# A graph network on one core: the stores of a sort's steps spread over its stream, the node figures' distance raised by one place, and the order of the first part left to the scheduler

## The chip, the cores and the metric

The kernel runs on one core of a Trainium2 chip. The time is the device time of one execution in microseconds; lower is better. Engines are named as the profile names them: PE is TensorE, DVE is VectorE, ACT is ScalarE, POOL is GpSimd, SP is SyncE. SP issues all of this kernel's transfers.

## What is computed

The input is sixteen graphs of N = 1024 nodes with C = 64 columns each, x, and an adjacency adj of 1024 by 1024. Four layers follow each other, each with a residual and a normalisation over the 64 columns. The first one costs nearly everything: it thins the adjacency ("dilation"), and then takes for every node and every column three quantiles over the node's remaining neighbours, with weights.

```python
def _dilate_adj(adj, mask):
    nb = (adj_ > 0) & (~eye)[None]
    m = nb.sum(-1)
    rank = jnp.cumsum(nb, axis=-1) - 1
    skip = jnp.where(m > T_THRESH, (m + K_DIL - 1) // K_DIL, 1)
    removed = nb & do_dil[..., None] & ((rank + 1) % skip[..., None] == 0)
    rem = removed | jnp.swapaxes(removed, 1, 2)
    return jnp.where(rem, 0.0, adj_)
...
for tau, wt in zip([0.25, 0.5, 0.75], [0.25, 0.5, 0.25]):
    pos = jnp.clip(tau * (mf - 1.0), 0.0)
    lo, hi = floor(pos), ceil(pos)
    q = gather(lo) * (1.0 - frac) + gather(hi) * frac     # of the sorted neighbours
    agg = agg + wt * q
...
x = _layernorm(x + _L0_gnn_ref(x, adj, nodemask, ...), axis=-1)
x = _layernorm(x + _L1_gnn_ref(x, adj, ...), axis=-1)      # three rounds of adj^T (x W)
x = _layernorm(x + _L2_gnn_ref(x, adj, ...), axis=-1)      # adj x / degree
x = _layernorm(x + _L3_gnn_ref(x, adj), axis=-1)           # (adj + I) x / sum
```

## The kernel before

**How the quantiles are found.** The kernel sorts the 1024 values of each column once and then counts: for six wanted ranks of each node it finds, by matmuls of the thinned adjacency with words that encode each value's place, in which block of 16 sorted values the rank falls, and then which value within it. The work unit (`Unit`) is one group of eight columns' words and one half of the nodes. A graph has 8 groups and 2 halves, so 16 units, and each unit has S = 6 turns, one for each wanted rank. In a turn VectorE makes a mask `mt` and a product `pr` (`masks`), TensorE sums them (`pw`, then `pr_`, `pv`, `fc`), ScalarE evacuates. Meanwhile TensorE counts for the next unit (`x` from `vt` and the words `xw`) and makes the next words (`pa` from `prow`). At the end of a group `total` reduces with the matmuls `p<-wv`.

**What runs beside it.** Four kinds of other work are written as Python generators, with a `yield` between their steps:

- `sort_pair` sorts the columns of two graphs at once (two graphs of 64 columns fill the 128 partitions). It is a bitonic network of 55 steps on VectorE; each step makes the comparison `m`, stores it to DRAM (`swaps`) and makes min and max. Then it takes differences of the sorted values ("the steps"), as float16 and a remainder, into a tile `both`, and stores that tile to DRAM with eight transfers (line 419). Then it lays out 0 to 1023 with an iota `ii` (line 427), copies it to `sr`, and runs the 55 steps backward, with each `m` loaded again, so that `sr` ends as the rank of each value. Those ranks become the rows that the words are made of.
- `dilate` thins one graph's adjacency: for each of eight tiles a threshold and a prefix sum (`sc`), six small POOL operations for the node figures `sk` (lines 515 to 520), two ACT passes that use `sk`, three VectorE operations; then transposes, row sums (`pm`) and the six ranks per node (`rd`).
- `degrees` sums the columns, by ACT, through one buffer `ac`.
- `layers` does the rest of the network for the graph before, with loads `a` of 512 KB through three buffers.

**What sets the order.** The main loop goes over `y`, one turn at a time, and each turn has two places. `Spread` puts the generators' steps into the places. A generator with so many `steps` between `first` and `end` has an even schedule, and `late` says how many places it is behind. `ready` lets a step wait until it is four places late (`LATE`) as long as VectorE's planned work, `Ordered.through`, is more than `BUSY` ahead of the place's time, `Ordered.now`; the kernel adds a fixed formula per VectorE instruction to `through`. A digit in what a generator yields is a distance: the next step comes at least so many places after this one. Letters: "p" is a use of TensorE, "v", "n", "h" limit which steps may share a place.

`Ordered` also chains each instruction of VectorE and ScalarE to the one written before it, without a wait, as `link` does for TensorE, so that their order is as written. SP and POOL aren't chained, and the scheduler of the framework orders them. While `Ordered.on` is false, VectorE and ScalarE are ordered by that scheduler too, and `through` isn't counted.

**The first part.** Before the main loop the first sort, the dilation of graph 0, its rows and its first words must be done. `Ordered.on` is set to true ahead of them. Dilation goes on by one step at every second step of the backward sort, and then at each word part.

**Buffers.** All tiles of a sort (`sv`, `both`, `ii`, `sr`, `sb`) share one tag with two buffers, and so `sr` is given the buffer of `both`; `m` has two buffers of its own.

```python
        both = sorts.tile([P, 2 * N], F16, tag="s", name="sv")
...
        ii, _, _ = slot("ii")
...
        _, r, d = slot("sr")
        V.tensor_copy(r, ii)
```

Of the kernel before, what the change touches and what calls it, by code (L numbers as in the profile page):

```python
# [37 lines left out]
def gnn_stack(  # L38
# [322 lines left out]
    def sort_pair(b, rows, found):  # L361
# [52 lines left out]
        for u in range(TURN):  # L414
            for c2 in range(2):
                q0 = (u * 2 + c2) * (C // 2)
                for i in range(2):

                    nc.sync.dma_start(
                        out=xs[u].rearrange("(b e) q i c f -> e i c q b f", e=2)[c2, i, c2],  # L420
                        in_=both[q0 : q0 + C // 2, ts(i, N)].rearrange("q (b f) -> q b f", f=F),
                    )
        found.append((xs, back))
        yield
        ii, _, _ = slot("ii")
        ii = ii.bitcast(I32)
        nc.gpsimd.iota(ii, pattern=[[1, N]], base=0, channel_multiplier=0)
# [51 lines left out]
    def dilate(g, found):  # L479

        mk = small.tile([P, T], F32, tag="mk", name="mk")
        V.tensor_copy(mk, mask8[:, g, :])
        den = small.tile([P, 2, T], F32, tag="den", name="den", bufs=3)
        vt = graph.tile([P, T, N], F16, tag="vt", name="vt", bufs=2)

        def block_of(t):
            a = []
            for h in range(2):
                a.append(strm.tile([P, HALF], F32, tag="da", name="da", bufs=2))
                nc.sync.dma_start(out=a[h], in_=adj[g, ts(t, P), ts(h, HALF)])  # L490
            return a

        a = block_of(0)
        yield
        for t in range(T):
            sc = dil.tile([P, 2 * N], F16, tag="d", name="sc")
            nb, cum = sc[:, 0:N], sc[:, N : 2 * N]
            q = vt[:, t, :]
            for h in range(2):
                V.tensor_scalar(nb[:, ts(h, HALF)], a[h], 0.0, None, ALU.is_gt)  # L500
                A.activation(
                    q[:, ts(h, HALF)], a[h], AF.Copy, accum_out=den[:, h, t : t + 1]
                )
            if t + 1 < T:
                a = block_of(t + 1)
            V.tensor_tensor(nb[:, ts(t, P)], nb[:, ts(t, P)], offdiag, ALU.mult)

            V.tensor_tensor_scan(cum, nb, nb, 0.0, ALU.add, ALU.max)
            yield
            m = cum[:, N - 1 : N]  # L510


            sk = small.tile([P, 5], F32, tag="sk", name="sk")
            G = nc.gpsimd
            G.tensor_scalar(sk[:, 0:1], m, 0.5, 0.5, ALU.add, ALU.mult)  # L515
            G.tensor_scalar(sk[:, 0:1], sk[:, 0:1], MAGIC, -MAGIC, ALU.add, ALU.add)
            G.tensor_scalar(sk[:, 1:2], m, T_THRESH, mk[:, t : t + 1], ALU.is_gt, ALU.mult)
            G.tensor_scalar(sk[:, 2:3], sk[:, 0:1], 1.0, sk[:, 1:2], ALU.add, ALU.mult)
            G.tensor_scalar(sk[:, 3:4], sk[:, 2:3], -1.5, 1.5, ALU.mult, ALU.add)
            G.tensor_scalar(sk[:, 4:5], sk[:, 2:3], 0.5, -0.5, ALU.mult, ALU.add)  # L520
            yield "4"

            for h in range(2):
                A.activation(
                    q[:, ts(h, HALF)], cum[:, ts(h, HALF)], AF.Abs, bias=sk[:, 3:4]
                )
                yield "2"
            V.tensor_scalar(q, q, sk[:, 4:5], 0.25, ALU.is_equal, ALU.max)
            V.tensor_tensor(q, q, nb, ALU.mult)
            V.scalar_tensor_tensor(  # L530
                q[:, ts(t, P)], ident16, 0.25, q[:, ts(t, P)], ALU.mult, ALU.add
            )
            yield
        yield

        tiles = vt.rearrange("p j (t m) -> p j t m", m=P)
        for j in range(T):
            for t0 in range(j + 1, T, 4):
                yield PEV
                n = min(4, T - t0)  # L540
                pq = bank(ps_l, "pq", dt=F16).rearrange("p (i t m) -> p i t m", i=2, m=P)
                for i in range(n):
                    transpose(pq[:, 0, i], tiles[:, t0 + i, j], ident16)
                    transpose(pq[:, 1, i], tiles[:, j, t0 + i], ident16)
                for i, side in enumerate((tiles[:, j, t0 : t0 + n], tiles[:, t0 : t0 + n, j])):
                    V.scalar_tensor_tensor(
                        side, pq[:, i, 0:n], 0.25, side, ALU.is_equal, ALU.is_gt
                    )
        yield PEV
        pq = bank(ps_l, "pq", dt=F16).rearrange("p (t m) -> p t m", m=P)  # L550
        for j in range(T):
            transpose(pq[:, j], tiles[:, j, j], ident16)
        side = bass.AP(vt.tensor, vt.offset, [list(vt.ap[0]), [N + P, T], [1, P]])
        V.scalar_tensor_tensor(side, pq, 0.25, side, ALU.is_equal, ALU.is_gt)
        yield

        rd = dram.tile([S, N], F16, name="rd")
        wd = dram.tile([S, N], F16, name="wd")
        yield PEV
        pm = bank(ps_l, "pm")  # L560
        for t in range(T):
            for j in range(T):
                matmul(
                    pm[:, t : t + 1], lhsT=vt[:, j, ts(t, P)], rhs=one16[:, 0:1],
                    start=(j == 0), stop=(j == T - 1), skip_group_check=True,
                )

        def wide_of(i):
            return by_s[:, i].unsqueeze(1).to_broadcast([P, T, S])

        pos = small.tile([P, T, S], F32, tag="pos", name="pos", bufs=1)
        nb1 = small.tile([P, T], F32, tag="nb1", name="nb1", bufs=1)
        rw = small.tile([P, T, 2 * S], F16, tag="rw", name="rw", bufs=1)
        r, w = rw[:, :, 0:S], rw[:, :, S : 2 * S]
        V.tensor_scalar(nb1, pm[:, 0:T], -1.0, 0.0, ALU.add, ALU.max)
        V.tensor_tensor(pos, nb1.unsqueeze(2).to_broadcast([P, T, S]), wide_of(0), ALU.mult)
        V.tensor_scalar(r, pos, 1023.625, 1024.0, ALU.add, ALU.max)
        V.scalar_tensor_tensor(pos, pos, 1024.0, r, ALU.add, ALU.subtract)
        V.tensor_tensor(w, pos, wide_of(1), ALU.mult)
        V.tensor_tensor(w, w, wide_of(2), ALU.add)  # L580
        V.scalar_tensor_tensor(pos, pos, 0.0, wide_of(3), ALU.is_gt, ALU.mult)
        V.tensor_tensor(r, r, pos, ALU.add)
        yield "4" + PEN
        pq = bank(ps_l, "pq", dt=F16)
        for t in range(T):
            transpose(pq[0 : 2 * S, ts(t, P)], rw[:, t], ident16)
        sc = dil.tile([P, 2 * N], F16, tag="d", name="sc")
        A.copy(sc[0 : 2 * S, 0:N], pq[0 : 2 * S])
        nc.sync.dma_start(out=rd, in_=sc[0:S, 0:N])
        nc.sync.dma_start(out=wd, in_=sc[S : 2 * S, 0:N])  # L590
        found.append((vt, rd, wd, den))
# [480 lines left out]
            )  # L1072
        infos[g]["w96"] = w96

    Ordered.on = True
    sorting, dilating = sort_of(0, sorted_), dilate(0, parts)
    for i, _ in enumerate(sorting):
        if i == 0:  # L1080
            onerow = strm.tile([P, N], F32, tag="a", name="onerow").bitcast(F16)[0:C, 0:N]
            V.memset(onerow, 1.0)
            for r in rows_in:
                nc.sync.dma_start(out=r[4], in_=onerow)
            nothing = strm.tile([P, N], F32, tag="a", name="nothing").bitcast(F16)
            V.memset(nothing, 0.0)
            for r in steps_in:
                for u in range(TURN):
                    nc.sync.dma_start(
                        out=r[u].rearrange("p q i c f -> p (q i c f)"), in_=nothing  # L1090
                    )
        if i > n_sort and i % 2:
            next(dilating, None)
    load_rows(rows_of(0), 0)
    load_rows(rows_of(0), 1)
    words = {0: {}}
    for k in range(KC):
        words[0][k] = wts.tile([P, 2, T, P], F16, tag="xw", name="xw")
        for part in range(4):
            word_part(0, words[0][k], k, part)  # L1100
            next(dilating, None)
            if part % 2:
                word_end(words[0][k], part // 2)
            next(dilating, None)
    all_of(dilating)
    info(0)
    for s in range(S):
        load_rank(0, s)
# [70 lines left out]
    for y in range(n_units * S + S):  # L1179
# [4 lines left out]
        if running and z == 0:  # L1184
# [2 lines left out]
            base = 2 * SLOTS * g  # L1187
            if g == 0 and TURN < B:
                background.append(
                    Spread(sort_of(1, sorted_), 2 * n_sort + 8, 0, base + 2 * SLOTS + ROWS)  # L1190
                )
            if g + 1 < B:
                background.append(Spread(dilate(g + 1, parts), 64, base, base + 168))
# [33 lines left out]
        for half in range(2):  # L1227

            if running:
# [3 lines left out]
                if g % TURN and place == base + ROWS and g + 3 < B:  # L1233

                    background.append(
                        Spread(
                            sort_of((g + 3) // TURN, sorted_), 2 * n_sort + 8, place,
                            place + 4 * SLOTS,
                        )
                    )  # L1240
# [74 lines left out]
```

## Time and profile before

| | us |
|---|---|
| median of three runs | 9303.98 (9301.11 to 9304.25) |
| the profiled execution | 9303.79 |
| its span, first to last instruction | 9302.0 |
| PE busy | 8584.0 |
| DVE busy | 8194.6 |
| ACT busy | 7165.3 |
| POOL busy | 1064.4 |

The mean granted clock of TensorE is 0.990. In the profile, a group is named by what it writes and reads (`pr<-mt,dw`), with the buffer numbers left out. Nearly all operations of VectorE and ScalarE carry the line of the helper in `Ordered` (L299) and those of TensorE that of `link`'s callers (L280, L277), so they are told apart by their tiles. A wait is given with the instruction that stood idle, what ended its idle time, the total in us, how often, and the longest. An instruction in order of time has its start, its length, and in brackets the idle time ahead of it. A row of a stretch of time has the busy time of PE, PEld, DVE, ACT and POOL with the number of instructions, then the granted clock, the DMA share and GB/s.

The sixteen graphs are spread evenly: with the matmuls `p<-wv` as marks, the second to the fourteenth graph take 546.7 to 559.8 us each.

### The profile page before, as it was taken

Reading aid. Unit: us, or ns where it says so; the run is one execution under the profiler, and the core shown is the slowest. Engines: PE = TensorE matmul, PEld = TensorE weight load, DVE = VectorE, ACT = ScalarE, POOL = GpSimd, SP = SyncE. Lnnn points to the kernel's source line nnn. Section 1 sums busy time; section 2 is a strip of 40 time slices with the busy share of each in tenths; the row PEclk is TensorE's granted clock in tenths of the full one; section 3 lists DMA queues with packets and bytes.
Section 4 is the critical chain, followed back from the end, with each engine's and each line's share of the span. In section 5 each row is a group of like instructions: output and inputs, shape, how many; then the busy total and the mean of one; then the engine's idle time right before and its main releaser. Section 6 shows DMA issues by size and latency. Waiting matters only on the chain.

```text
span 9302.0 us, 188268 instructions
## 1 busy us (share of the span) xinstructions
PE 8584.0 (92%) x78785; PEld 3692.7 (40%) x78785; DVE 8194.6 (88%) x8786; ACT 7165.3 (77%) x12465; POOL 1064.4 (11%) x923
## 2 busy tenths in 40 slices
PE   0689999999999999999999999999999999999997
PEld 0234444444444444444444444444444444444442
DVE  8799989989899998989999898998989899777663
ACT  0588878878787887878888787887878788887873
POOL 0110101101020110201112010210102111010000
PEclk9999999999999999999999999999999999999998
DMA  3111222222222222222222222222222222221111
GB/s 93 53 39 42 78 88 66 81 70 92 76 77 69 77 75 83 82 78 64 92 68 87 76 78 80 73 77 72 94 73 80 69 72 81 67 66 65 44 62 56
DMA packets 531942, 678.39 MB, mean 73 GB/s; under 512 B 234576, under 2 KB 349392, under 8 KB 531088
## 3 DMA queue, kind: packets, MB, share of 16 engines
q1 hardware_dynamic: 531088, 666.35, 23.4%
q8 instruction: 616, 10.09, 0.4%
q14 instruction: 238, 1.95, 0.1%
HBM read 584.36 MB, written 81.80 MB: 72 GB/s over the span
## 4 chain that ended last, share of the span: by engine, by line
PE 62%; DVE 22%; ACT 7%; issue 7%; DMA 1%; POOL 1%; SPq 1%; another core or an unknown queue 0%; DVEq 0%; POOLq 0%; ACTq 0%
PE x L280 27%; PE pa L280 10%; PE pw L280 9%; PE pv L280 7%; DVE pr L299 6%; DVE mt L299 5%; PE fc L280 3%; DVE sr L299 3%; ACT dw L299 3%; DVE sv L299 2%; DVE vt L299 1%; PE p L280 1%; ACT xw L299 1%; DVE sc L299 1%; DVE m L299 1%
## 5 line engine op out<-in xcount | busy, mean ns | idle before, releaser
L280 PE MATMUL x<-vt,xw 128*128 128x512 f16 x16384 | 3988.9, 381 | 102.7 <-ACT dw L299 99.4
L299 DVE TENSOR_TENSOR pr<-mt,dw 128x4096 f16<-128x4096 f16 x1536 | 3520.5, 2292 | 72.5 <-ACT dw L299 1.0
L299 DVE TENSOR_TENSOR mt<-cc,rB 128x2048 f16<-128x2048 f16 x1536 | 1871.6, 1218 | 677.4 <-PE pv L280 651.3
L280 PEld LDWEIGHTS <-xw 128*128 128x128 f16 x16384 | 1500.7, 98 | 1727.9 <-issue 419.0
L299 ACT ACTIVATE qq<-pw,col,icol 128x512 f16<-128x512 f32 x1536 | 1212.1, 789 | 776.4 <-PE pw L280 744.7
L299 ACT ACTIVATE xw<-pa 128x512 f16<-128x512 f32 x2048 | 1247.3, 609 | 471.2 <-PE pa L280 470.5
L299 ACT ACTIVATE dw<-x 128x512 f16<-128x512 f32 x2048 | 1119.3, 604 | 279.2 <-PE x L280 270.2
L299 ACT ACTIVATE xw<-xw 128x1024 f16<-128x1024 f16 x1024 | 1088.7, 1063 | 11.0
L280 PE MATMUL pa<-words_by,prow 128*128 128x128 f16 x8192 | 805.7, 221 | 306.8 <-DMA prow<-rows 283.1
L280 PEld LDWEIGHTS <-prow 128*128 128x128 f16 x8192 | 557.4, 98 | 1161.5 <-issue 670.0
L280 PE MATMUL pw<-pr,red 128*32 128x512 f16 x12288 | 932.4, 380 | 45.9 <-DVE pr L299 45.8
L299 ACT ACTIVATE val<-pv 128x512 f32<-128x512 f32 x1536 | 938.0, 611 | 6.4 <-PE x L280 5.0
L280 PE MATMUL pv<-mt,txw 128*32 128x512 f16 x12288 | 933.0, 380 | 0.0
L755 POOL TENSOR_TENSOR rstd<-var,neghalf 128x8 f32<-128x8 f32 x112 | 212.5, 1897 | 4223.2 <-DVE var L299 4223.2
L299 ACT ACTIVATE cc<-x 128x512 f16<-128x512 f32 x1024 | 613.2, 599 | 92.1 <-PE x L280 88.0
L280 PE MATMUL pw<-rB,subr 128*32 128x512 f16 x6144 | 615.2, 390 | 0.6 <-ACT qq L299 0.3
L299 DVE TENSOR_TENSOR sr<-sr 128x512 f16<-128x512 f16 x1336 | 598.6, 477 | 17.4
L280 PE MATMUL pv<-nt,nbig 128*32 128x512 f16 x6144 | 599.9, 380 | 0.0
L299 DVE TENSOR_TENSOR sv<-sv 128x512 f32<-128x512 f32 (+3 forms) x904 | 595.1, 698 | 0.6
L280 PE MATMUL fc<-val,fin 128*32 128x512 f32 x3072 | 528.0, 593 | 0.0
L515 POOL TENSOR_SCALAR sk<-sc 128x1 f32<-128x1 f16 x128 | 84.9, 663 | 3386.9 <-DVE sc L299 2310.7
L280 PEld LDWEIGHTS <-txw 128*32 128x32 f16 x12288 | 330.8, 97 | 335.0 <-issue 2.9
(3288 smaller groups left out, 8421.7 us busy)
## 6 DMA issues: line engine op xcount, KB each, us to landing
a<-adj_dram SPq DMA_DIRECT2D x360, 512.0 KB
a<-adjT_dram SPq DMA_DIRECT2D x240, 512.0 KB
da<-adj_dram SPq DMA_DIRECT2D x256, 256.0 KB
ac<-adjT_dram SPq DMA_DIRECT2D x256, 256.0 KB
swaps<-m SPq DMA_DIRECT2D x440, 128.0 KB
m<-swaps SPq DMA_DIRECT2D x440, 128.0 KB
rB<-rd SPq DMA_DIRECT2D x96, 256.0 KB
prow<-rows SPq DMA_DIRECT2D x512, 20.0 KB
```

Source lines behind the costliest of these rows:

```text
L280: link("PE", nc.tensor.matmul(*args, **kw))
L299: ins = call(*args, **kw)
L515: G.tensor_scalar(sk[:, 0:1], m, 0.5, 0.5, ALU.add, ALU.mult)
L755: nc.gpsimd.tensor_tensor(rstd, var, neghalf, ALU.pow)
```

## The change

There are three parts.

1. In `sort_pair` each pair of stores of `both` is followed by a `yield`, so that the eight stores make four steps in place of one, and the step with the iota comes with a distance of "4" behind the last pair. The number of steps that `Spread` reckons with goes from 2 n_sort + 8 to 2 n_sort + 12 (n_sort is 55).
2. In `dilate` the distance behind the node figures goes from "4" to "5", and the end of a tile gets a distance of "1".
3. In the first part, `Ordered.on` isn't set ahead of the sort (the main loop sets it), the first sort runs through, the first dilation is written behind it as a whole, and the word parts come without steps of dilation among them.

```diff
@@ sort_pair
                         in_=both[q0 : q0 + C // 2, ts(i, N)].rearrange("q (b f) -> q b f", f=F),
                     )
+                yield
         found.append((xs, back))
-        yield
+
+        yield "4"
         ii, _, _ = slot("ii")
@@ dilate
-            yield "4"
+            yield "5"
...
-            yield
+            yield "1"
         yield
@@ the first part
-    Ordered.on = True
-    sorting, dilating = sort_of(0, sorted_), dilate(0, parts)
-    for i, _ in enumerate(sorting):
+    for i, _ in enumerate(sort_of(0, sorted_)):
...
-        if i > n_sort and i % 2:
-            next(dilating, None)
+    all_of(dilate(0, parts))
     load_rows(rows_of(0), 0)
     load_rows(rows_of(0), 1)
...
             word_part(0, words[0][k], k, part)
-            next(dilating, None)
             if part % 2:
                 word_end(words[0][k], part // 2)
-            next(dilating, None)
-    all_of(dilating)
     info(0)
@@ the main loop, twice
-                    Spread(sort_of(1, sorted_), 2 * n_sort + 8, 0, base + 2 * SLOTS + ROWS)
+                    Spread(sort_of(1, sorted_), 2 * n_sort + 12, 0, base + 2 * SLOTS + ROWS)
```

More of the change, by code (lines that the diff above doesn't have):

```diff
@@ L1236, in gnn_stack @@
                         Spread(
-                            sort_of((g + 3) // TURN, sorted_), 2 * n_sort + 8, place,
+                            sort_of((g + 3) // TURN, sorted_), 2 * n_sort + 12, place,
                             place + 4 * SLOTS,
```

## The prediction

> **What bounds the kernel now.** I read the page first, then the waits of TensorE and VectorE over the steady part (360 to 9220 us), then the instructions in order of time at the places where those waits fall, then the first 351 us in the same way, and last the granted clock in slices of 5 us.
>
> ```profile
> PE 8584.0 (92%) x78785; PEld 3692.7 (40%) x78785; DVE 8194.6 (88%) x8786; ACT 7165.3 (77%) x12465; POOL 1064.4 (11%) x923
> PE   0689999999999999999999999999999999999997
> DVE  8799989989899998989999898998989899777663
> ```
> The slices say that TensorE is the bound from the second one on, with VectorE close behind; before that TensorE is idle. So two things can be worth something: holes in TensorE's steady work, and the time before it starts.
>
> ```profile
> DVE mt L299 <- PE pv L280: 651.3, 450, 4.1
> DVE sr L299 <- DMA ac<-adjT_dram: 37.7, 4, 9.5
> DVE sr L299 <- DMA steps<-sv: 28.4, 3, 9.5
> ```
> These are VectorE's largest waits in the steady part. The first is slack (it waits for TensorE). The next two are one thing under two names: four and three times, each 9.4 us, the copy sr<-ii stands still. The order of this instruction lists all eight store semaphores as what it waits for, and the two buffers of tag "s" say why: sr takes the buffer that the stores of the steps still read.
>
> ```profile
> PE pw L280 <- DVE pr L299: 45.8, 40, 7.6
> PE pq L277 <- DVE msg L299: 44.1, 6, 7.8
> ```
> TensorE's answer: once 7.6 us behind pr, six times 7.4 us behind msg. Both names are only what stood behind the waiting copy on VectorE.
>
> ```profile
> 818.55 9.66 SPq L419 DMA_DIRECT2D steps<-sv  x8
> 820.95 2.29 DVE L299 TENSOR_TENSOR pr<-mt,dw 128x4096 f16<-128x4096 f16 x1
> 832.67 0.69 DVE L299 CAST sr<-ii 128x1024 f16<-128x1024 int32 x1 [9.43 <-DMA steps<-sv]
> 839.41 1.04 PE L280 MATMUL pw<-pr,red 128*32 128x512 f16 x8 [7.57 <-DVE pr L299]
> ```
> One such place, from three engines: eight stores take the queue 9.66 us, end at 828.2, the last lands by 832.67 (4.5 us later), VectorE is idle from 823.2, TensorE 7.57 us.
>
> ```profile
> 2976.00:2981.00 5.00, 0.00 (x0) 0.00 (x0) 4.90 (x6) 0.96 (x2) 0.00 (x0) 0.61 0.62 225
> 2981.00:2986.00 5.00, 3.29 (x14) 1.65 (x14) 4.96 (x5) 0.60 (x1) 0.00 (x0) 0.50 0.00 0
> ```
> The clock (third number from the end) falls to 0.50 behind the hole, so a hole costs more than its length.
>
> ```profile
> 151.57 0.69 DVE L299 CAST sr<-ii 128x1024 f16<-128x1024 int32 x1 [14.40 <-DMA steps<-sv]
> 289.11 0.48 DVE L299 TENSOR_SCALAR vt<-vt,sk 128x1024 f16<-128x1024 f16 x1
> 301.54 0.49 DVE L299 TENSOR_SCALAR vt<-vt,sk 128x1024 f16<-128x1024 f16 x1 [7.64 <-ACT vt L299]
> 350.89 1.23 DVE L299 TENSOR_TENSOR mt<-cc,rB 128x2048 f16<-128x2048 f16 x1 [16.61 <-ACT cc L299]
> ```
> The first part: the sort is done at 289.1, but dilate is not (its pieces at 289 and 301), so the first mask of the main loop comes at 350.89. VectorE is busy 274.8 of these 350.9 us.
>
> **What the Trainium skill says.** "Perfetto Trace Analysis", section "Tensor Engine Instruction (MATMUL, LD_WEIGHTS)": ACT, DVE and GPSIMD are strict FIFO. The trace agrees: mt for the next mask is ready to run at 823 and stands behind the copy until 835.8. "TensorE: Matmul & The Clock Gate", Part 1, "What's actually happening": after an idle window the array runs at half clock until it has been busy for a window. Agrees: 0.50 after the 7.7 us hole at 2975. "DMA: Bandwidth & Descriptors", "Issuing engines are not separate DMA queues": all transfers share the same engines. Here all of them are also issued by SP in one order (every row of the DMA issues says SPq), so a store's place in that order matters.
>
> **The change part by part.**
>
> *Stores spread, then four places.* Nothing is added or dropped; eight stores become four steps of two, and the iota and sr<-ii come at least four places after the last pair. A place is half a mask's turn: 192 places per graph, and the graphs take 550 to 560 us, so 2.9 us. Steps of the sort stand some three places apart. Last pair: two issues of 1.2 us and 4.5 us of landing, 6.9 us, against 11.6 us of distance. The wait goes, with 4.7 us to spare; what hides the stores is the masks in between, and without that cover 9.4 us come back each time. Gain per place: 7.4 us of hole; then the cold clock: behind the hole at 2975 six x matmuls take 2.77 against 1.47 elsewhere, five 1.85 against 1.24, four pa 0.63 against 0.39, four pq some 0.2 more, together 2.35. Sum 9.75. A second way: the time from the matmuls p<-wv of one group of columns to those of the next (eight groups to a graph) is 79.5 us on the mean of the six where a copy stands and 70.6 at the same place of the next graph, where there is none: 8.9. I take 9.3 between the two, seven times: -65 us (bounds 52, the holes alone, and 68). Behind the wait nothing is late: TensorE is 98% busy before and after. On SP the pairs now stand between loads a (for the layers) and ac; a store behind such a load may come late, since SP waited up to 11.0 us for an ac buffer near these places. I allow +4 (bounds 0 and 30). Sort steps go from 118 to 122 over the same 384 places: same instructions, 0.
>
> *Five places, and one at a tile's end.* sk's six small POOL operations take 2.2 us (159.76 to 161.91). ACT's wait for sk is 262.4 us in all, 259.4 of it in the first part, so 3.0 us are left for the loop: gain 0 (bounds -3 and +2). The tiles' average distance is 13 places and the waits now sum to 10, so nothing piles up at the end.
>
> *First part, order left open.* Without the links, the scheduler takes dilate's pieces in between the forward sort's steps; most of its transposed groups land between `both` and sr<-ii, so they fill the 14.4 us wait for stores; all 16 word parts come behind the sort, then x. VectorE work until the sort's last row: 274.8, plus 1.4 of memsets that came after the first mask. Idle that I expect within: 3.3 at the start, 8 between pq transposes (8.7 before), 3.6 for the rows store (3.55 before), and 9 for swaps that come late, since loads of da, constants, rB and w96 now stand among them in SP's order (7.1 of such waits before). Sum 300, against 289. From there: 6.5 us to the first pa (289.2 to 295.7 before), eight pairs of word parts at 2.07 on ACT (two at 0.53, one whole at 1.0), in whose shadow the first x starts at about +15.5, and 14.8 us from first x to first mask (336.1 to 350.9). First mask at 337 instead of 351: -14 us (bounds -4 with ten more of late swaps, -20).
>
> *A side effect of that.* `Ordered.on` also fed the planner's counter `through`. Adding up its formula over the first part, before starts the loop some 259,000 ns ahead of `now`, above BUSY until about place 1440 of 3072: till then every background step waits until it is four places late. After starts near zero, so the whole loop runs as before's second half does, the layers four places earlier. Before has both regimes: the iotas of successive sorts are 1109.9 and 1109.5 us apart in the first, 1109.9 and 1111.4 in the second. Cost +3 (bounds -3 and +10).
>
> Sum against the profiled execution (span 9302.0, time 9303.8, the median of three 9304.0): 9303.8 - 65 + 4 + 0 - 14 + 3 = 9232.
>
> **Rivals.**
> 1. *The store wait stays in part*, because SP reaches the last pair late behind ac or a. For it: SP's waits of 5 to 11 us there. Against: such loads are waited for by what the same place of the program frees. With 4 us left in each of seven sorts, 28 in place of the 4 allowed: 9256.
> 2. *The first part gains nothing*: swaps loads late at each of the 55 backward steps. For: rd, rB and w96 in their midst. Against: ten such steps ran at 1.71 us each without a wait at 160 to 173. First mask near 355: 9250.
> 3. *The planner costs*: with steps taken early, VectorE's pieces bunch. For: alternate graphs in the second half are 551 to 553, in the first 550 to 551. At +8 a graph over the eight graphs of the first half, 64 in place of 3: 9293, no change.
> 4. *Slower: the spread stores hold up the layers' loads.* SP is one order; in six sorts four pairs stand among the a loads, which TensorE's pa needs in its own order. If each of the 24 pairs makes pa wait for its 2.4 us of issue and 2.35 of cold clock, 114 more: 9346. It decides from 3.8 us a pair (91 us, to 0.2% above before). Against: TensorE has no wait for a in before, though there the queue is held for 9.66 us at once, and three buffers lie ahead.
> 5. That the change doesn't do what it says: the order of the changed program does show pairs, and sr<-ii behind them; small.
>
> **How the numbers follow.** Forecast 0.68, rival 1 0.12, 2 0.08, 3 0.06, 4 0.06. The range takes the bounds of the forecast (9303.8 - 68 - 20 - 3 gives 9213) and reaches over rivals 1 and 2: 9212 to 9264. About 0.2% (19 us) is what a measurement tells from no change: faster 0.88 (forecast, 1, 2), within 0.06 (3), slower 0.06 (4).
>
> **What would show it.** sr<-ii without a wait above 1 us seven times, no 7 us row of pq behind msg, no clock below 0.9 there, the first mask at 331 to 347, graphs all at 549 to 553. It is wrong if the copy still waits several us, if pa waits for a, if the first mask comes after 351, or if the steady graphs grow.

## The result and the profile after

| | before | after |
|---|---|---|
| median, us | 9303.17 (9301.11 to 9304.25, four runs) | 9223.34 (9222.42 to 9227.07, four runs) |
| profiled execution | 9303.79 | 9223.88 |
| its span | 9302.0 | 9222.1 |
| mean granted clock of TensorE | 0.990 | 0.994 |
| first mask of the main loop starts at | 350.89 | 341.54 |

The ratio of the times is 0.9915, with a 95% interval of 0.9898 to 0.9932. The change saves 79.8 us; forecast were 72 (9232, range 9212 to 9264). All times here and below are of executions with a mean granted clock of 0.989 or more; one execution of part 1 with the counter at zero, 22641.38 us long at a clock of 0.581, is left out.

The page after, engines and two of the rows of slices:

```profile
PE 8569.1 (93%) x78785; PEld 3685.2 (40%) x78785; DVE 8187.5 (89%) x8786; ACT 7160.6 (78%) x12465; POOL 1084.5 (12%) x923
PE   0599999999999999999999999999999999999996
DVE  8899999999898999989999898998989999777663
```

The counts of instructions are those of before, and the busy times of PE and DVE are within 0.2%. So the 80 us are idle time and clock, not work. PE's third slice was at 8 before and is at 9 now.

The largest waits of VectorE, 340 to 9140 us (instruction, what ended the wait, total us, times, longest):

```profile
DVE mt L299 <- PE pv L280: 643.1, 472, 4.1
DVE x L299 <- POOL rstd L757: 51.8, 29, 1.8
DVE mt L299 <- ACT cc L299: 35.0, 1, 35.0
```

No line of sr<-ii is left: the two rows with 37.7 and 28.4 us are gone. The 35.0 us are one wait, that of the loop's first mask, shown below; x behind rstd had 36.2 us in 30 waits before. The rest of the list has no row above 14 us.

The waits of TensorE in the same stretch:

```profile
PE x L280 <- ACT dw L299: 101.1, 411, 0.2
PE x L280 <- ACT cc L299: 41.1, 74, 2.0
...
PE pw L280 <- DVE pr L299: 28.6, 20, 3.0
PE pq L277 <- DVE vt L299: 27.1, 48, 1.9
```

The row of pq behind msg (44.1 us, six times) is gone, and the longest wait behind pr is 3.0 in place of 7.6 us. What is late now is many times and little: pq behind vt had 11.4 us in 15 waits before, x behind cc 17.9 in 23. No row has TensorE waiting for a load `a`.

One sort's stores in the order of SP (start, length, issue, how many in a row), and the same place on VectorE:

```profile
2910.93 1.58 SPq L419 DMA_DIRECT2D steps<-sv  x2
...
2914.29 4.51 SPq L419 DMA_DIRECT2D steps<-sv  x2
2918.90 1.22 SPq L785 DMA_DIRECT2D a<-adjT_dram  x1
2920.16 4.21 SPq L419 DMA_DIRECT2D steps<-sv  x3
2924.46 1.76 SPq L785 DMA_DIRECT2D a<-adjT_dram  x2
2926.32 0.37 SPq L816 DMA_DIRECT2D ac<-adjT_dram  x1
2926.74 0.42 SPq L419 DMA_DIRECT2D steps<-sv  x1
```

```profile
2910.94 1.22 DVE L299 TENSOR_TENSOR sv<-sv 128x1024 f16<-128x1024 f32 x1
...
2952.60 1.22 DVE L299 TENSOR_TENSOR mt<-cc,rB 128x2048 f16<-128x2048 f16 x1 [1.38 <-PE pv L280]
...
2957.20 0.68 DVE L299 CAST sr<-ii 128x1024 f16<-128x1024 int32 x1
```

Two things are to be seen. The copy sr<-ii has no bracket, so it waits for nothing; that is so at all seven copies of the loop. And the stores are hardly spread: written as four steps of two, they leave SP within 16 us, between a few loads, and the first of them leaves as the last instruction that makes `both` starts (2910.94). SP isn't chained, so its order is the scheduler's. What is moved is VectorE's copy in its stream: it comes at 2957.20, 30 us after the last store has left.

The granted clock at this copy, and where the same sort's copy had its hole before (columns as before; the clock is the third number from the end):

```profile
2955.00:2960.00 5.00, 4.74 (x78) 2.09 (x76) 4.90 (x7) 4.61 (x10) 0.00 (x0) 1.00 0.18 52
2960.00:2965.00 5.00, 5.00 (x77) 2.71 (x76) 4.76 (x8) 3.06 (x5) 0.00 (x0) 1.00 0.13 36
...
2975.00:2980.00 5.00, 5.00 (x54) 2.66 (x53) 3.79 (x7) 4.84 (x10) 0.00 (x0) 1.00 0.11 31
2980.00:2985.00 5.00, 5.00 (x50) 2.00 (x48) 3.15 (x4) 4.35 (x7) 1.64 (x1) 1.00 0.08 20
```

The first part on VectorE: the copy, the sort's last row, and the first mask of the main loop; and VectorE's waits from 0 to 343 us:

```profile
190.93 0.69 DVE L299 CAST sr<-ii 128x1024 f16<-128x1024 int32 x1
...
305.80 0.69 DVE L299 TENSOR_TENSOR sr<-sr 128x1024 uint16<-128x1024 f16 x1
341.54 2.36 DVE L299 TENSOR_TENSOR mt<-cc,rB 128x2048 f16<-128x2048 f16 x2 [35.04 <-ACT cc L299]
```

```profile
DVE vt L299 <- ACT vt L299: 16.4, 7, 2.9
DVE vt L299 <- PE pq L277: 7.2, 9, 1.1
DVE sr L299 <- DMA rows<-sr: 3.1, 2, 2.3
...
DVE m L299 <- DMA swaps<-m: 1.4, 1, 1.4
```

The 14.4 us ahead of the copy are gone; dilate's transposes stand there. The sort ends at 306.5 with all of dilate done, and from there to the first mask VectorE only waits (35.04 us).

With the matmuls `p<-wv` as marks, the sum over graphs falls in both halves of the loop. All sums by stretch below are made in this way, each from one profiled execution:

| us | to the first mark | graph 0 | graphs 1 to 7 | graphs 8 to 13 |
|---|---|---|---|---|
| before | 441.8 | 529.8 | 3883.4 | 3327.2 |
| after | 435.0 | 523.4 | 3850.4 | 3293.8 |

### The profile page after: what moved, and what is told of

It reads as the page before. It is cut to its first block, busy times and chain, and to the rows that moved or that the text cites. A ratio compares the mean times of both kernels' runs of the same rounds, so it can differ in the third digit from the quotient of the medians.

```text
span 9222.1 us, 188186 instructions
## 1 busy us (share of the span) xinstructions
PE 8569.1 (93%) x78785; PEld 3685.2 (40%) x78785; DVE 8187.5 (89%) x8786; ACT 7160.6 (78%) x12465; POOL 1084.5 (12%) x923
## 4 chain that ended last, share of the span: by engine, by line
PE 68%; DVE 15%; ACT 9%; issue 7%; POOL 1%; DMA 1%; SPq 0%; another core or an unknown queue 0%; POOLq 0%; DVEq 0%; ACTq 0%
PE x L280 30%; PE pa L280 10%; PE pw L280 10%; PE pv L280 7%; PE fc L280 4%; DVE pr L299 4%; DVE mt L299 3%; ACT dw L299 3%; DVE sr L299 3%; DVE sv L299 2%; ACT xw L299 2%; ACT qq L299 1%; PE p L280 1%; DVE vt L299 1%; PE pc L280 1%
## 5 line engine op out<-in xcount | busy, mean ns | idle before, releaser
L517 POOL TENSOR_SCALAR sk<-sc 128x1 f32<-128x1 f16 x128 | 112.7, 880 | 3579.5 <-DVE sc L299 2413.7
```

## The experiments

Twelve versions were run. Each is compared with runs of the kernel before in the same batch, whose median was 9304.24 (first four), 9304.61 (next four), 9305.55 (next three) and 9305.29 us (the last). Four runs were taken of a version where no other number is given.

**Part 1 alone.** The kernel before with the four yields, the "4" and 122 steps.

```diff
+                yield
         found.append((xs, back))
-        yield
+
+        yield "4"
```

> Before with the first part of the change alone (pairs of stores, a distance of 4 places, 122 steps). If the waits of sr<-ii are what the change removes: seven waits gone in the loop (the one in the first part stays, 14 us), 9303 - 65 = 9238, between 9234 and 9245. If the planner's counter is the real source: about 9285 or more.

Measured: 9236.36 us (9235.35 to 9238.17), ratio 0.9926 (0.9911 to 0.9941), 68 us faster. Graphs 1 to 7 take 3860.2 and graphs 8 to 13 take 3293.3 us: 23.2 and 33.9 less than before. Not all of it is the seven waits: 2.9 us come before the first mark (438.9 against 441.8), since the copy of the first part waits 11.57 in place of 14.40 us. Most of the change's gain is this part.

**Part 3 alone.** The first sort and dilation unlinked, stores and dilate as before.

```diff
-    Ordered.on = True
-    sorting, dilating = sort_of(0, sorted_), dilate(0, parts)
-    for i, _ in enumerate(sorting):
+    for i, _ in enumerate(sort_of(0, sorted_)):
...
+    all_of(dilate(0, parts))
```

> Before with the third part of the change alone: order of the first part left open, and with it the planner's counter near zero when the loop starts. First mask at 341 as in the changed kernel, 9 us earlier. If the counter costs or brings nothing: 9303 - 9 = 9294; if the counter brings the rest of what the waits and the first mask do not explain (some 6 to 8 us): 9287; if it costs 3: 9297. The seven waits of 9.4 us are all there.

Measured: 9307.33 us (9305.86 to 9308.86, twelve runs), ratio 1.0002 (0.9993 to 1.0011): no change. The first mark comes 9.1 us earlier (432.7), and the rest gives it back: graph 0 takes 3.7, graphs 1 to 7 take 5.3 and graphs 8 to 13 take 3.4 us more. So the part does more than move the start. The candidate for the rest is the planner's counter, which starts from about zero here, since `Ordered.on` was false during the first part.

**The change with the counter kept.** The changed kernel with the counter set, ahead of the main loop, to about what it was before.

```diff
+    Ordered.through = 262021.0
     wvs, background, resident = {}, [], ()
```

> The changed kernel with the planner's counter set to 262,021 ns ahead of the loop, the value at which the kernel before enters it; nothing else. If the counter is worth nothing: 9223, same as the changed kernel within 3. If running steps early costs (my +3): 9220. If it is what brought the odd graphs' 2 to 3 us: 9230.

Measured: 9246.00 us (9245.29 to 9246.87), ratio 0.9936 (0.9921 to 0.9951), 23 us slower than the change. In the change the side effect of the first part is a gain, against the +3 of the forecast. Graphs 8 to 13, where this counter too has fallen under BUSY, take 3292.3 us as in the change (3293.8); graphs 1 to 7 take 3872.3 against 3850.4.

**Distance without spreading.** The eight stores in one step as before, with a distance of six places behind them.

```diff
         found.append((xs, back))
-        yield
+        yield "6"
```

> Before with the eight stores in one step as they were, and a distance of 6 places (17 us) ahead of the iota in place of none. 9.7 us of issue and 4.5 of landing make 14.2, so the wait should be gone without spreading. If the wait on VectorE is all that counts: 9238, as with the spread stores. If the spreading itself matters (SP's queue held for 9.7 us, transfers colliding): 5 to 30 us slower than that.

Measured: 9262.11 us (9252.60 to 9263.44), ratio 0.9951 (0.9936 to 0.9966): 42 us faster, where part 1 as it is brought 68. VectorE waits for these stores once in the whole loop, for 0.7 us. So the waits in the loop went without any spreading, and still 26 us are missing. Graphs 1 to 7 take 3860.4 us, just as with part 1 alone (3860.2); graphs 8 to 13 take 3320.0, against 3293.3. One place of the second half, SP, VectorE and TensorE in order of time, and then the slices:

```profile
6247.05 12.11 SPq L419 DMA_DIRECT2D steps<-sv  x8
```

```profile
6266.29 0.68 DVE L299 CAST sr<-ii 128x1024 f16<-128x1024 int32 x1
...
6267.73 0.42 DVE L299 TENSOR_TENSOR sr<-sr,m 128x512 f16<-128x512 f16 x1
...
6270.04 0.42 DVE L299 TENSOR_TENSOR sr<-sr,m 128x512 f16<-128x512 f16 x1
...
6271.18 1.22 DVE L299 TENSOR_TENSOR mt<-cc,rB 128x2048 f16<-128x2048 f16 x1
```

```profile
6275.77 1.01 PE L277 MATMUL pq<-ident,vt 128*128 128x128 f16 x8 [2.97 <-DVE vt L299]
```

```profile
6270.00:6275.00 5.00, 2.80 (x33) 1.07 (x33) 4.90 (x7) 3.65 (x6) 0.00 (x0) 0.99 0.10 26
6275.00:6280.00 5.00, 4.23 (x20) 2.31 (x20) 4.97 (x6) 1.40 (x4) 0.00 (x0) 0.50 0.00 0
6280.00:6285.00 5.00, 4.98 (x49) 1.69 (x48) 3.10 (x7) 3.40 (x7) 0.00 (x0) 0.83 0.27 82
```

The copy and two backward steps (two pieces sr<-sr,m) stand ahead of one mask; from vt at 6265.62 to the mask at 6271.18 that is 5.6 us of VectorE's time, TensorE runs dry, and its clock falls to 0.50. A yield counts as a step of the schedule, a digit does not: here the sort waits six places with its schedule running on, and makes up for it by two steps in a row. That reading follows from how `late` is worked out and fits the order; it wasn't tried by itself with the number of steps changed, and it isn't the whole of the 26 us. The same order stands in the first half too (from vt at 2965.39 to the mask at 2970.96, 5.6 us), where nothing is lost against part 1. What differs is TensorE's hole behind it, here at the copy of 2966.06:

```profile
2975.03 0.62 PE L277 MATMUL pq<-ident,vt 128*128 128x128 f16 x8 [1.81 <-DVE vt L299]
```

A hole of 1.81 us there leaves the clock at 1.00; the three of 2.97 and 2.98 us in the second half each have a slice of 0.50 to 0.76 behind them. And of the 26.7 us only 18.6 lie in the three graphs that hold a copy. Where the others come from is open.

**Dilate's distances alone, and the change without them.**

```diff
-            yield "4"
+            yield "5"
...
-            yield
+            yield "1"
```

> Before with the second part of the change alone: distance 5 behind the node figures and 1 at a tile's end, the planner's counter as before far ahead for the first half. My prediction: nothing, 9304. The theory formed from the run with the counter kept (it is 10 slower than the spread alone although its first mask is earlier): this part costs some 1.7 us a graph while the counter is ahead, so graphs 1 to 7 are 12 us longer in sum, and nothing afterwards: 9316.

> The changed kernel without the second part (distance 4 and none at a tile's end). If the second part is without effect once the counter starts near zero: 9223. If it brings something: 9230 or more. If it costs there too: 9211.

Measured: alone 9307.73 us (9306.12 to 9311.79, twelve runs), ratio 1.0005 (0.9996 to 1.0013). The change without part 2: 9223.20 us (9221.74 to 9224.31), ratio 0.9914 (0.9899 to 0.9929), against 9223.34 with it. In these two settings part 2 is worth nothing, as forecast.

**The change without the "4" behind the last pair.**

```diff
-        yield "4"
+        yield
```

> The changed kernel with the stores in four steps, and no distance of 4 behind the last pair. The sort's steps stand three places apart (8.7 us), the last pair needs 6.9, so if only the wait counts: 9223, sr<-ii without a wait. If the distance is what removes the wait: a wait of 1 to 4 us in each of seven sorts, 9230 to 9250.

Measured: 9223.54 us (9220.63 to 9228.22), ratio 0.9915 (0.9900 to 0.9930), and the copy shown above comes at 2957.11 in place of 2957.20 us. The "4" doesn't bind. Between the instruction that finishes `both` and the copy lie five yields, at 384 places over 122 steps, 3.1 places each; with 2.9 us a place that is 46 us, and 2910.94 to 2957.20 is 46.3.

**Counting early: a version past the change.** The changed kernel, with the first unit's counting begun behind the first two of four tiles of words, and with half of each word finished by VectorE in place of ScalarE.

```diff
+    _, counting = unit_of(0)
     for k in range(KC):
...
-                word_end(words[0][k], part // 2)
+                V.tensor_scalar(whole, whole, -1.0, 1.0, ALU.mult, ALU.add)
+                V.tensor_scalar(whole, whole, 0.0, None, ALU.max)
+        if k:
+            all_of(itertools.islice(counting, 17))
```

> The changed kernel with another first part: the first unit's counting on TensorE begins behind the first two of its four word tiles in place of behind all of them, and the second half of a word (1 minus it, cut at 0) is made by VectorE, idle there for 35 us, in place of ScalarE. First mask at 332 to 335 in place of 341.5; if the time from the first mask to the end stays: 9215. If the loop's start only waits for something else: 9223.

Measured: 9220.08 us (9218.86 to 9221.22), ratio 0.9911 (0.9894 to 0.9927), the fastest version run, and 3 us under the change. In order of time, the first x of the changed kernel, and then the first x and the first mask of this version:

```profile
325.93 5.66 PE L280 MATMUL x<-vt,xw 128*128 128x512 f16 x16 [0.84 <-ACT xw L299]
```

```profile
316.39 3.87 PE L280 MATMUL x<-vt,xw 128*128 128x512 f16 x16
```

```profile
334.40 2.36 DVE L299 TENSOR_TENSOR mt<-cc,rB 128x2048 f16<-128x2048 f16 x2 [4.37 <-ACT cc L299]
```

The first mask comes 7.1 us earlier than the change's 341.54, and 3 us of it arrive at the end. That it beats the kernel before is certain; against the change the intervals of the two ratios overlap, and the 3 us alone don't settle it.

**What the counter is worth.** Three more runs complete the table of counter and stores: the change without dilate's distances with the counter kept (`Ordered.through = 262021.0`), part 1 alone with the counter at zero (`Ordered.through = 0`), and part 3 alone with the counter kept.

> The changed kernel without the second part (distances of dilate as before) and with the planner's counter set to 262,021 ns ahead of the loop. With the second part it measured 9246. If dilate's distances cost 12 just where the counter is ahead and the stores are spread: 9234. If the 12 come from the first part: 9246.

> Before with the stores spread, and the planner's counter set to 0 ahead of the loop; first part and dilate as before. The spread alone measured 9236. If the counter brings its gain together with the spread stores (10 over graphs 1 to 7): 9226. If it brings nothing by itself: 9236.

> Before with the first part's order left open, and the planner's counter set to 262,021 ns ahead of the loop. With the counter near zero it measured 9307. If the first part brings its 8 and the counter cost 11 where the stores are not spread: 9296. If the first part's gain is lost by itself in the loop: 9304 to 9307.

Measured: 9230.59 (9230.25 to 9233.77), ratio 0.9919 (0.9905 to 0.9934); 9229.53 (9228.77 to 9229.58, three runs), ratio 0.9917 (0.9897 to 0.9937); 9295.04 (9289.86 to 9300.01, twenty runs), ratio 0.9990 (0.9983 to 0.9996).

| us | counter ahead | counter from about zero | from about zero is |
|---|---|---|---|
| stores as before, first part unlinked | 9295.04 | 9307.33 | 12 slower |
| part 1, first part as before | 9236.36 | 9229.53 | 7 faster |
| parts 1 and 3 | 9230.59 | 9223.20 | 7 faster |
| parts 1, 2 and 3 | 9246.00 | 9223.34 | 23 faster |

The differences of 7 us are smaller than the intervals of the ratios (14 us either way and more), and those of the first row overlap a little. They rest on the runs themselves: in none of the four pairs do the two ranges of times overlap.

The first and the third row differ in part 1 alone, and the sign turns with it. The waits of TensorE from 340 to 9070 us show where the time goes. Part 3 alone, counter kept:

```profile
PE pw L280 <- DVE pr L299: 36.6, 34, 8.0
PE pa L280 <- ACT xw L299: 15.2, 27, 2.1
PE pq L277 <- DVE vt L299: 11.4, 16, 3.0
```

Part 3 alone, counter from about zero:

```profile
PE pw L280 <- DVE pr L299: 58.6, 50, 8.3
PE pa L280 <- ACT xw L299: 6.3, 19, 0.7
PE pq L277 <- DVE vt L299: 5.7, 10, 1.3
```

Steps taken early save 8.9 us at pa and 5.7 at pq here, but pw behind pr costs 22.0 more. With the stores spread that last term is gone: from 9230.59 to 9223.20 us, pa behind xw goes from 15.7 to 7.1, pq behind vt from 36.5 to 27.0, and pw behind pr only from 26.9 to 27.8. The layers' pc behind y takes part of that back, with 31.6 in place of 21.0.

Why pw behind pr grows where the stores are as before stays open. It doesn't grow at the waiting copies: the one such wait at a copy is 8.0 us with the counter kept and 8.3 from about zero. Of the 22.0 us, 7.6 lie in graph 0 and 13.0 in graphs 1 to 7, there in pieces of 1.6 us at most. Nor is it shown that the wait for the stores is what turns the sign: part 1 also gives the sort four more steps, and so other places for all of them, and no run has the waits gone at 118 steps with the counter at zero. Nearest to it is the second half of the distance of six, where the counter has fallen: no copy waits there, and it is 26.7 us longer than with part 1.

The last row of the table is larger by dilate's distances: with the counter ahead they cost 15 us (9230.59 to 9246.00), with it at zero none.

**Always late.** The change without dilate's distances, with the counter so high that each background step waits until it is four places late in the whole loop (`Ordered.through = 1.0e9`).

> The changed kernel without dilate's distances, the planner's counter set so far ahead (a second) that every step waits until it is four places late in the whole loop, not only in its first half. With the first half late it measured 9231, with none 9223. If being late costs some 1.7 to 2 us a graph: 12 more over graphs 8 to 14, 9243. If the 7 us belong to something that happens once (the change from one way to the other, or the loop's start): 9231 or less.

Measured: 9247.28 us (9245.71 to 9249.70), ratio 0.9940 (0.9923 to 0.9957), 24 us slower than the same kernel with the counter from about zero. Graphs 1 to 7 take 13.7 us more (3860.0 against 3846.3), and so do graphs 8 to 13 (3309.6 against 3295.9). With the counter at 262021 only the first of the two stretches was longer (3860.8 and 3291.4). So with the stores spread it is the waiting until late that costs, wherever in the loop it holds.

## Why the prediction was right, point by point

- **The bound.** Right: busy times and counts stayed, and 80 us of holes, cold clock and start went.
- **The stores.** The forecast had -65, with +4 for SP. Part 1 alone gives -68, at the upper bound of 68, and the four us of lateness did not come: the copy waits for nothing. Of the 68, 2.9 are the first part's shorter wait, which the forecast has under the first part. The reason given was wrong in part. The last pair was reckoned to leave where it is written, with four places and 4.7 us to spare. In the trace all four pairs leave within 16 us behind `both`, five yields ahead of the copy; of the 30 us from the last store's issue to the copy the landing (4.5 us before) takes a part, and some 25 are to spare. That the stores needn't be apart for it, the distance of six shows: with all eight in one row the wait is gone too.
- **The cold clock.** Counting it beside the hole (7.4 + 2.35) was right in size: 65 us of the loop over seven places are 9.3 each, and the seven graphs that hold a copy are by themselves 60.9 us shorter, 8.7 each. Both are more than the hole alone.
- **Dilate.** 0 was forecast; 0 in the change and a difference within the interval alone. It is not free under every order: 15 us with the counter ahead and the stores spread, outside the bounds of -3 and +2.
- **The first part.** -14 was forecast, with the first mask at 337; it comes at 341.54, 9.4 us early, and with the counter kept part 3 is worth 6 (9236.36 to 9230.59) to 10 us (9295.04 against 9305.55) in the end. From the sort's end to the mask the sum was good: 36.8 reckoned, 35 measured. The step that failed is the idle time ahead of it. Its terms were 3.3 for the start, 8 for the transposes, 3.6 for the rows store and 9 for swaps, 23.9 in all; VectorE's list of waits gives 3.4, 8.1, 3.1 and 2.0 for these, and 16.4 for a term that was left out: vt waits for ScalarE within dilate. That row was in sight before, with 10.8 us in two waits; the sum took none of it over. So the sort ends at 306.5 and not at 300.
- **The planner.** +3 was forecast, with bounds of -3 and +10; it is -7 in parts 1 and 3, and -23 beside part 2. This is the one step with the wrong sign. It was read from the two halves of the kernel before, and in both of them the copy waits for the stores: the first and third rows of the table above give +12 and -7 for the same edit. A side effect was priced in the state that the change removes; which part of that state turns the sign isn't shown.
- **Rivals.** Store wait in part (9256): no, the copy has no wait. First part worth nothing (9250): no, 6 to 10. Planner costs (9293): true only for part 3 by itself, where it takes the whole gain of the first part. Slower by late loads `a` (9346): no row of pa behind a load stands among TensorE's waits.
- **The signs named ahead.** The copy without a wait seven times, no row of pq behind msg, a full clock at the copies, a first mask within 331 to 347: all there. Graphs 1 to 13 take 546.4 to 552.7 us, against 549 to 553: the last one, with 546.4, is below, as it was before (546.7), and four others miss 549 by half a us at most.

In sum: -68 for the stores, -6 for the first part, -7 for the counter and 0 for dilate are -81 when they are added in this order, beside -79.8 measured and -72 forecast. Against the forecast the stores are 7 better (with their allowance), the planner 10 better and the first part 8 worse: errors of both signs. That the total is nearer than its steps is luck; within part 3 the two misses all but cancel (-11 forecast, -13 measured beside the spread stores, 9236.36 to 9223.20).

## What to carry to other kernels

Where an in-order engine waits for stores that read a buffer it wants again, put the distance into that engine's stream. Here steps of the schedule were worth 26 us more than a bare distance. How the stores themselves are written may not survive a scheduler. A planner's setting must be priced together with the rest of the change: here the same edit was worth +12 us with the stores as before and -7 with part 1. An experiment that does each part alone is not enough for that; the pairs are needed.

## What the hardware showed beside this

Short holes can cool TensorE too. In the changed kernel, outside any copy, the layers' pc waits 2.57 us for VectorE, and the next slice has a clock of 0.66:

```profile
4790.78 1.55 PE L280 MATMUL pc<-center,y 128*128 128x128 f32 x8 [2.57 <-DVE y L299]
```

```profile
4785.00:4790.00 5.00, 3.21 (x39) 1.28 (x37) 4.93 (x5) 4.67 (x9) 0.00 (x0) 1.00 0.00 0
4790.00:4795.00 5.00, 4.22 (x19) 2.69 (x20) 4.96 (x6) 2.14 (x3) 0.00 (x0) 0.66 0.12 39
```

0.66 over 5 us would be 3.4 us at half clock, 1.7 us of loss for a hole of 2.57. The same goes with pc at 5890.43 (a hole of 2.70, a slice at 0.66), and the two slices with a hole of 2.00 at 6421.66, of 0.79 and 0.87, come to 1.7 us as well; pc at 5340.98, with a hole of 1.07 and the clock at 1.00, takes 1.13 us in place of 1.55. But not every such hole does it: of the nine of 2.00 to 2.97 us between 360 and 9000 us, seven have such a loss and two, 2.71 at 477.74 and 2.49 at 2594.57, keep 1.00. In these nine the length of the hole doesn't tell which. So the places of 2 us and more that are left in the change are on the whole dearer than their row of waits says; no run took them away.
